# A chain of transformer layers: the score buffers in PSUM as single banks instead of pairs of banks

## The chip, the cores and the metric

The kernel runs on one core of a Trainium2 chip. The metric is the device time of one execution. The kernel before took 545.48 us (median of three runs, 543.8 to 546.18). The profiled execution that all traces below come from has a span of 545.9 us. Engines are called by their names in the profile: PE is TensorE (PEld its weight loads), DVE VectorE, ACT ScalarE, POOL GpSimd, SP the queue that issues DMA.

## The reference, cut to what matters

The input x has 8 sequences of 256 tokens with 128 features, all float32. Eight residual blocks follow each other, each on the layernorm of x:

```
x = x + causal_attention(ln(x))      # one head
x = x + ffn_relu(ln(x))
x = x + linear_attention(ln(x))
x = x + ffn_relu(ln(x))
x = x + retention(ln(x))             # 16 heads
x = x + ffn_silu(ln(x))
x = x + softmax_attention(ln(x))     # 16 heads of 8 features
x = x + ffn_silu(ln(x))
```

The change concerns the softmax attention of 16 heads:

```
scores = einsum('bhqd,bhkd->bhqk', q, k) / sqrt(8)
attn = softmax(scores)
ctx = einsum('bhqk,bhkd->bhqd', attn, v)
out = ctx @ Wo.T + bo
```

So there are 8 sequences x 16 heads, each with a 256 x 256 matrix of scores.

## The kernel before, in words

**Groups.** The 8 sequences are cut into 4 groups of 2. Each group walks through all layers (`layers`, L1253) as a thread of its own, and the groups start a little apart, so that at any time different groups are in different layers and their work mixes on the engines. The last group ends alone.

**Who sets the order.** The order of instructions is worked out in Python, before anything runs, by `Plan` (L111). Every piece of work is a generator that yields steps such as `step(DVE, 1.15)`: an engine and a booked time in us. The planner holds a clock for each engine, adds a handoff time when work goes from one engine to another, and always emits the step that can start first; among those that could start, the thread with the lower rank goes first (group 0 ahead of group 3; the scores of the softmax attention, rank -1, ahead of all). The booked times decide only the order of instructions in each engine's queue. On the chip each engine works through its queue in that order and waits on semaphores for its data and buffers.

**Buffers.** Buffers lie in stores. A thread that wants one yields `get(store, n)` and gets it when the planner thinks that it is free; `put` gives it back, with `later=LEEWAY` 0.4 us after the planned end. PSUM has eight banks of 512 float32 columns for each partition. Before the change they are four tiles of two banks, the twins (L338); all other work takes single halves of twins from the store `bank` (L340).

**Scores.** `pairs_of_scores` (L1026) is one endless thread that serves all softmax attentions. Scores are computed twice: first with queries on the partitions, to find the maximum of each row (`firsts`), and then, with the negative maximum joined to the operands as one more row, with keys on the partitions, for the exponential (`seconds`). The unit is a pair of heads, `(seq, h2)`: two matmuls for each head, one for each 128 rows of its score matrix, so four in all. They are float32, and each shows as two records in the profile, so a pair is x8 at L1070. Each uses 32 rows of the array. A head's rows, `place(h)` (L1023), are one of four groups of 32 rows; a pair takes two of them. A step of the planner takes one pair (a lone step) or two pairs on different rows, booked with 0.8 us of PE either way (L1065).

While other groups are under way, two twins are lent to the scores, and a step with two pairs waits for both (L1056). Once the last group is in its softmax attention, `todo["alone"]` is set, a third twin is lent (L1036), and a step takes the first twin that comes free. A second pair joins only if another twin is free at that moment (L1060); otherwise it goes back to its queue.

**After the scores.** `maxima` (L1085) takes the negative maximum of both heads with one DVE instruction over the whole twin, 1024 columns, and gives the twin back. After four pairs, the maxima are transposed, copied and sent by DMA into the rows of the operands, and the four pairs go to `seconds`. `exponentials` (L1119) takes the exponential of both heads with one ACT instruction over the twin, into a buffer `probs`, and gives the twin back. `weighted` (L1128) multiplies the probabilities of four pairs with the values (L1140); the column of ones in the values gives the sums of the softmax. When all is done for a sequence, the output projection (L1237) and the second `ffn_silu` follow, for that sequence alone.

Of the kernel before, what the change touches and what calls it, by code (L numbers as in the profile page):

```python
# [27 lines left out]
F32 = mybir.dt.float32  # L28
I32 = mybir.dt.int32
AF = mybir.ActivationFunctionType  # L30
ALU = mybir.AluOpType
AX = mybir.AxisListType

P = 128
B, S, D = 8, 256, 128
GROUPS = 4
NT = 4
N = NT * P
# [22 lines left out]
PE, ACT, DVE, POOL, SP = "pe", "act", "dve", "pool", "sp"  # L61
# [3 lines left out]
LEEWAY = 0.4  # L65
# [45 lines left out]
class Plan:  # L111
# [18 lines left out]
    def spawn(self, steps, rank=None):  # L130

        c = self.current
        th = Thread(steps, c.rank if rank is None else rank, c.t if c else 0.0, c.last if c else None)
        self.resume(th, None)
        return th
# [8 lines left out]
    def put(self, store, *items, later=0.0):  # L144
        for item in items:
            self.count += 1
            store.items.append((self.current.after() + later, self.count, item))
# [94 lines left out]
def step(engine, us, table=None):  # L242
    return ("step", ((engine, us, table),))
# [6 lines left out]
def get(store, n=1):  # L250
    return ("get", store, n)
# [6 lines left out]
def until(condition):  # L258
    return ("until", condition)


def wake(us):
    return ("at", us)
# [3 lines left out]
def hybrid(ctx: ExitStack, tc: tile.TileContext, t: dict, out: bass.AP):  # L267
    nc = tc.nc
    plan = Plan()
    put, spawn = plan.put, plan.spawn  # L270
# [3 lines left out]
    psum = ctx.enter_context(tc.tile_pool(name="psum", bufs=1, space=bass.MemoryType.PSUM))  # L274
# [4 lines left out]
    def buffers(name, n, shape):  # L279
        return plan.store([buffer(f"{name}{i}", shape) for i in range(n)])  # L280
# [54 lines left out]
    plan.free[POOL], plan.free[ACT] = 2.6, 2.6  # L335


    twins = [psum.tile([P, 2, N], F32, tag=f"twin{i}", name=f"twin{i}") for i in range(4)]  # L338
    halves = [[tw[:, k, :] for k in range(2)] for tw in twins]
    bank = plan.store([h for pair in halves for h in pair], strict=True)  # L340
    twin = plan.store([])
    work = buffers("work", 28, [P, WORK])
    small = buffers("small", 16, [P, P])
    probs = buffers("probs", 6, [P, 2, N])
# [15 lines left out]
    def flat(tl):  # L360
        return tl.rearrange("p a b -> p (a b)")
# [8 lines left out]
    def copied(dst, src, us):  # L370
        e = yield either((ACT, us), (DVE, us + 0.02))
        (nc.scalar.copy if e == ACT else nc.vector.tensor_copy)(dst, src)  # L372
# [644 lines left out]
        pass  # L1017

    firsts, seconds = deque(), deque()
    todo = {"sequences": 2 * GROUPS, "banks": [0, 1], "alone": False}  # L1020
    under_way = [0, 0]

    def place(h):  # L1023
        return slice(32 * (h % 4), 32 * (h % 4) + 32), h // 4

    def pairs_of_scores():  # L1026

        yield until(lambda: firsts)
        yield get(bank, halves[0] + halves[1])
        put(twin, *twins[:2])
        while todo["sequences"]:
            yield until(lambda: firsts or seconds or not todo["sequences"])
            if todo["alone"] and len(todo["banks"]) == 2:  # L1036
                yield get(bank, halves[2])
                put(twin, twins[2])
                todo["banks"].append(2)
            chosen = []  # L1040
            kinds = [(firsts, 0), (seconds, 1)]
            if todo["alone"] and under_way[0] > under_way[1]:
                kinds.reverse()
            for queue, of_keys in kinds + kinds:
                for n in range(min(2, len(queue))):
                    if len(chosen) == 2 or any(h2 % 2 == queue[n][1] % 2 for _, _, h2 in chosen):
                        continue
                    if n and queue[0][1] // 2 != queue[1][1] // 2:
                        continue
                    chosen.append((of_keys, *queue[n]))  # L1050
                    del queue[n]
                    break
            if not chosen:
                break
            if len(chosen) == 2 and not todo["alone"]:
                ps = yield get(twin, 2)  # L1056
            else:
                ps = [(yield get(twin))]
                if len(chosen) == 2:
                    if any(i[0] <= plan.now for i in twin.items):  # L1060
                        ps.append((yield get(twin)))
                    else:
                        of_keys, *pair = chosen.pop()
                        (seconds if of_keys else firsts).appendleft(tuple(pair))
            yield step(PE, 0.8)  # L1065
            for n in range(2):
                for k in range(2):
                    for (of_keys, seq, h2), to in zip(chosen, ps):
                        rows, j = place(2 * h2 + k)
                        nc.tensor.matmul(  # L1070
                            to[:, k, n * S : (n + 1) * S],
                            seq.spread[rows, j, of_keys, n * P : (n + 1) * P],
                            seq.spread[rows, j, 1 - of_keys, :], start=True, stop=True,
                        )
            for (of_keys, seq, h2), to in zip(chosen, ps):
                under_way[of_keys] += 1
                if of_keys:
                    seq.scored += 1
                    if seq.scored == HEADS // 2:
                        put(l_spread, seq.spread)  # L1080
                spawn((exponentials if of_keys else maxima)(seq, h2, to))
        yield get(twin, twins[: len(todo["banks"])])
        put(bank, *[h for n in todo["banks"] for h in halves[n]])

    def maxima(seq, h2, ps):  # L1085
        half = h2 // 4
        flat_nmax = seq.nmax[:, 16 * half : 16 * half + 16]
        nmax = flat_nmax.rearrange("p (j i m) -> p j i m", i=4, j=2)
        yield step(DVE, 1.15)
        nc.vector.tensor_reduce(  # L1090
            nmax[:, h2 % 4 // 2, 2 * (h2 % 2) : 2 * (h2 % 2) + 2, :],
            ps.rearrange("p k (m s) -> p k m s", m=2), AX.X, ALU.max, negate=True,
        )
        put(twin, ps, later=LEEWAY)
        under_way[0] -= 1
        seq.found[half] += 1
        if seq.found[half] < 4:
            return

        rows = yield get(small)  # L1100
        ps = yield get(bank)
        yield step(PE, 0.12)
        nc.tensor.transpose(ps[:16, :P], flat_nmax, ident)
        seq.turned += 1
        if seq.turned == 2:
            put(small, seq.nmax)
        yield from copied(rows[:16, :], ps[:16, :P], 0.25)
        put(bank, ps)
        for j in range(2):
            yield step(SP, 0.5)  # L1110
            nc.sync.dma_start(
                seq.spread[KDIM:P:32, 2 * half + j, 0, :], rows[8 * j : 8 * j + 8, :]
            )
        put(small, rows)
        yield wake(plan.current.after())
        seconds.extend((seq, 4 * half + n) for n in range(4))
        seq.parts.append(spawn(weighted(seq, half)))

    def exponentials(seq, h2, ps):  # L1119

        p = yield get(probs)
        yield step(ACT, 1.05, "exp")
        nc.scalar.activation(flat(p), flat(ps), AF.Exp)  # L1123
        put(twin, ps, later=LEEWAY)
        under_way[1] -= 1
        seq.p[h2] = (p, plan.current.after())

# [140 lines left out]
    plan.start(silu_weights(), LAST, 24.0)  # L1268
    plan.start(softmax_weights(), LAST, 24.0)
    plan.start(pairs_of_scores(), FIRST, 0.0)  # L1270
    plan.run()
    return plan
# [108 lines left out]
```

## Time and profile before

| What | Value |
|---|---|
| median of three runs | 545.48 us |
| span of the trace | 545.9 us |
| PE busy | 468.9 us, 86% |
| DVE busy | 343.6 us, 63% |
| ACT busy | 225.5 us, 41% |
| score matmuls L1070 | 1024 records, 99.3 us of PE |
| maxima L1090 | 64 instructions, 76.3 us of DVE |
| exponentials L1123 | 64 instructions, 63.4 us of ACT |
| first score matmul | at 210.8 us |
| mean granted PE clock | 0.934 of full speed |

A group's line in the profile gives line, engine, operation, destination <- sources, shapes and count; then the busy time in us and the mean of one instruction in ns; then how long the engine sat idle just before these instructions and which instruction released most of it. A line of a stage gives the stage, its length, the busy time of PE, PEld, DVE, ACT and POOL with the number of instructions in brackets, the granted PE clock as a share of full speed, and DMA. A line of the timeline gives the start and the length of a run of equal instructions, and their count at the end; idle time before it stands in square brackets. Line numbers are those of the kernel before. The helper `copied` records all its copies at L372.

### The profile page before, as it was taken

The numbers are of one execution on the slowest core, as the hardware profiler recorded it, in microseconds if no ns is written. First come the engines' busy times: TensorE is split into PE (matmuls) and PEld (weight loads), VectorE is DVE, ScalarE is ACT, GpSimd is POOL, SyncE is SP. The second block draws the span as 40 slices with busy tenths as digits, with TensorE's granted clock in tenths as the row PEclk, the third lists the DMA queues.
The fourth block names the chain that finished last, engine by engine and source line by source line (L and its number), as shares of the span: only waits on it lengthen the run. The fifth ranks groups of instructions, "written<-read, shape, count | busy, mean of one in ns | idle before, by whom it ended". The sixth has DMA issues, their size and how long they took to land. (4 is left out here: it accounts for less than half of the span.)

```text
span 545.9 us, 12836 instructions
## 1 busy us (share of the span) xinstructions
PE 468.9 (86%) x5340; PEld 316.8 (58%) x5340; DVE 343.6 (63%) x911; ACT 225.5 (41%) x414; POOL 146.1 (27%) x260
## 2 busy tenths in 40 slices
PE   2788799798889898899888788899779998989986
PEld 1676577566656666355654554556547565656555
DVE  6978774987795759776428874543876542752023
ACT  3235354432433242345443246435434664122362
POOL 6705476683352522415000120220001030000000
PEclk9979989999899989899989889989999999965599
DMA  8000000002002010002101002001000002000000
GB/s 297 37 2 1 1 1 1 0 18 26 3 14 27 3 42 2 1 2 40 25 3 22 2 18 24 3 22 24 2 1 22 10 13 41 11 1 11 2 0 20
DMA packets 8041, 10.88 MB, mean 20 GB/s; under 512 B 1000, under 2 KB 6888, under 8 KB 7984
## 3 DMA queue, kind: packets, MB, share of 16 engines
q1 hardware_dynamic: 7904, 9.94, 7.9%
q8 instruction: 42, 0.69, 0.6%
q14 instruction: 15, 0.12, 0.1%
q10 hardware_dynamic: 80, 0.13, 0.1%
HBM read 4.56 MB, written 1.05 MB: 10 GB/s over the span
## 5 line engine op out<-in xcount | busy, mean ns | idle before, releaser
L1070 PE MATMUL twin<-l_spread 32*128 32x256 f32 x1024 | 99.3, 443 | 3.9 <-DVE small L1090 3.3
L1090 DVE TENSOR_REDUCE small<-twin 128x4 f32<-128x1024 f32 x64 | 76.3, 1218 | 25.0 <-PE twin L1070 24.9
L470 POOL TENSOR_SCALAR small<-small 128x4 f32<-128x4 f32 (+1 forms) x44 | 10.4, 237 | 288.5 <-DVE small L468 287.5
L1123 ACT ACTIVATE probs<-twin 128x1024 f32<-128x1024 f32 x64 | 63.4, 1023 | 57.1 <-PE twin L1070 56.2
L372 ACT COPY work<-twin 128x512 f32<-128x512 f32 (+3 forms) x80 | 37.9, 481 | 114.4 <-PE twin L1140 30.5
L1070 PEld LDWEIGHTS twin<-l_spread 32*128 32x128 f32 x1024 | 62.7, 206 | 33.1 <-issue 15.3
L372 DVE COPY work<-twin 128x512 f32<-128x512 f32 (+3 forms) x32 | 17.6, 554 | 44.3 <-PE twin L1140 19.6
L1140 PE MATMUL twin<-probs,l_values 128*32 128x256 f32 x512 | 38.9, 444 | 7.2 <-DVE work L780 2.7
L472 POOL TENSOR_TENSOR small<-small,mhalf 128x4 f32<-128x4 f32 (+1 forms) x44 | 43.2, 982 | 0.0
L479 ACT ACTIVATE work<-x,small 128x128 f32<-128x128 f32 x74 | 32.3, 487 | 25.1 <-POOL small L473 24.9
L499 PE MATMUL twin<-ident,work 128*128 128x128 f32 x128 | 24.8, 299 | 16.8 <-ACT work L479 9.6
L467 DVE BATCH_NORM_STATS2 small<-x 128x6 f32<-128x128 f32 x128 | 34.5, 270 | 4.5 <-DMA x<-in_x 4.2
L484 DVE TENSOR_SCALAR work<-x,small 128x128 f32<-128x128 f32 x54 | 29.4, 765 | 6.3 <-POOL small L472 6.2
L468 DVE BATCH_NORM_AGGREGATE small<-small 128x2 f32<-128x6 f32 x160 | 29.1, 182 | 5.6
L659 PE MATMUL twin<-work,c_relu 128*128 128x512 f32 x64 | 30.5, 603 | 1.8 <-ACT work L372 1.8
L672 PE MATMUL twin<-c_relu,work 128*128 128x128 f32 x256 | 31.5, 277 | 0.1
L672 PEld LDWEIGHTS twin<-c_relu,work 128*128 128x128 f32 x256 | 30.1, 192 | 2.7 <-issue 1.4
L1140 PEld LDWEIGHTS twin<-probs,l_values 128*32 128x32 f32 x512 | 16.5, 123 | 25.5 <-issue 10.1
L499 PEld LDWEIGHTS twin<-ident,work 128*128 128x128 f32 x128 | 15.3, 145 | 27.2 <-ACT work L479 16.4
L985 PE MATMUL twin<-work,c_ints 128*128 128x256 f32 (+1 forms) x72 | 26.6, 489 | 4.3 <-ACT work L372 1.5
L1001 PE MATMUL twin<-c_ints,work 128*128 128x128 f32 x192 | 28.2, 294 | 2.0 <-DVE x L522 1.2
L991 PE MATMUL twin<-work,c_ints 128*128 128x256 f32 (+1 forms) x72 | 26.3, 485 | 2.8 <-DVE work L929 1.2
(145 smaller groups left out, 794.2 us busy)
## 6 DMA issues: line engine op xcount, KB each, us to landing
r_spread<-wide SPq DMA_DIRECT2D x32, 64.0 KB
l_spread<-wide SPq DMA_DIRECT2D x32, 64.0 KB
out<-x SPq DMA_DIRECT2D x8, 128.0 KB
c_retention_qk<-in_retention_qk SPq DMA_DIRECT2D x1, 770.0 KB
x<-in_x SPq DMA_DIRECT2D x3, 256.0 KB
c_retention_vo<-in_retention_vo SPq DMA_DIRECT2D x1, 713.0 KB
c_relu<-in_relu SPq DMA_DIRECT2D x1, 706.0 KB
c_ints<-in_ints SPq DMA_DIRECT2D x1, 576.0 KB
```

Source lines behind the costliest of these rows:

```text
L372: (nc.scalar.copy if e == ACT else nc.vector.tensor_copy)(dst, src)
L467: nc.vector.bn_stats(stats[:, i, :], src[:, i, :])
L472: nc.gpsimd.tensor_tensor(rstd, rstd, minus_half[:, :nt], ALU.pow)
L479: nc.scalar.activation(y[:, i, :], src[:, i, :], AF.Identity, bias=shift[:, i : i + 1], scale=rstd[:, i : i + 1],)
L484: nc.vector.tensor_scalar(y[:, i, :], src[:, i, :], mv[:, i, 0:1], rstd[:, i : i + 1], ALU.subtract, ALU.mult,)
L499: nc.tensor.transpose(ps[:, i * P : (i + 1) * P], y[:, i, :], ident)
L659: nc.tensor.matmul(ps, w1[:, c * P : (c + 1) * P], yT[:, :N], start=True, stop=True)
L672: nc.tensor.matmul(ps[:, n * D : (n + 1) * D], h[c][:, i * P : (i + 1) * P], w2[:, c, :], start=(c == 0), stop=(c == 3),)
L1070: nc.tensor.matmul(to[:, k, n * S : (n + 1) * S], seq.spread[rows, j, of_keys, n * P : (n + 1) * P], seq.spread[rows, j, 1 - of_keys, :], ...
L1090: nc.vector.tensor_reduce(nmax[:, h2 % 4 // 2, 2 * (h2 % 2) : 2 * (h2 % 2) + 2, :], ps.rearrange("p k (m s) -> p k m s", m=2), AX.X, ALU.m ...
L1123: nc.scalar.activation(flat(p), flat(ps), AF.Exp)
L1140: nc.tensor.matmul(o[32 * i : 32 * (i + 1), (j % 2) * S : (j % 2 + 1) * S], seq.v[:, c, VONE * h : VONE * h + 32], seq.p[h2][0][:, k, c * ...
```

## The change

The four twins become eight tiles of one bank each. A pair of heads now gets two such tiles, any two, one for each head. The maximum and the exponential are taken by one instruction for each head, of 512 columns instead of 1024, and each gives its bank back as soon as it has ended, instead of both together. The lending changes from two (later three) twins to four (later six) banks: outside the tail a step with two pairs waits for four banks; in the tail a step waits for two, and a second pair joins if two more are free at that moment. What it is for: finer buffers, so that a bank is not held for the sake of its neighbour, and a reader can start when one head is there. The planner's booked times go from 1.15 to 2 x 0.61 us for a maximum and from 1.05 to 2 x 0.6 us for an exponential. The matmuls, their order inside a step, and the arithmetic stay as they are.

```diff
-    twins = [psum.tile([P, 2, N], F32, tag=f"twin{i}", name=f"twin{i}") for i in range(4)]
-    halves = [[tw[:, k, :] for k in range(2)] for tw in twins]
-    bank = plan.store([h for pair in halves for h in pair], strict=True)
-    twin = plan.store([])
+    banks = [psum.tile([P, N], F32, tag=f"bank{i}", name=f"bank{i}") for i in range(8)]
+    bank = plan.store(banks, strict=True)
+    score_bank = plan.store([])
...
-            if todo["alone"] and len(todo["banks"]) == 2:
-                yield get(bank, halves[2])
-                put(twin, twins[2])
-                todo["banks"].append(2)
+            if todo["alone"] and todo["banks"] == 4:
+                yield get(bank, banks[4:6])
+                put(score_bank, *banks[4:6])
+                todo["banks"] = 6
...
             if len(chosen) == 2 and not todo["alone"]:
-                ps = yield get(twin, 2)
+                ps = yield get(score_bank, 4)
             else:
-                ps = [(yield get(twin))]
+                ps = yield get(score_bank, 2)
                 if len(chosen) == 2:
-                    if any(i[0] <= plan.now for i in twin.items):
-                        ps.append((yield get(twin)))
+                    if sum(i[0] <= plan.now for i in score_bank.items) > 1:
+                        ps = ps + (yield get(score_bank, 2))
                     else:
...
+            ps = [ps[n : n + 2] for n in range(0, len(ps), 2)]
...
-                            to[:, k, n * S : (n + 1) * S],
+                            to[k][:, n * S : (n + 1) * S],
...
     def maxima(seq, h2, ps):
-        yield step(DVE, 1.15)
-        nc.vector.tensor_reduce(
-            nmax[:, h2 % 4 // 2, 2 * (h2 % 2) : 2 * (h2 % 2) + 2, :],
-            ps.rearrange("p k (m s) -> p k m s", m=2), AX.X, ALU.max, negate=True,
-        )
-        put(twin, ps, later=LEEWAY)
+        for k in range(2):
+            yield step(DVE, 0.61)
+            nc.vector.tensor_reduce(
+                nmax[:, h2 % 4 // 2, 2 * (h2 % 2) + k, :],
+                ps[k].rearrange("p (m s) -> p m s", m=2), AX.X, ALU.max, negate=True,
+            )
+            put(score_bank, ps[k], later=LEEWAY)
...
     def exponentials(seq, h2, ps):
-        yield step(ACT, 1.05, "exp")
-        nc.scalar.activation(flat(p), flat(ps), AF.Exp)
-        put(twin, ps, later=LEEWAY)
+        for k in range(2):
+            yield step(ACT, 0.6, "exp")
+            nc.scalar.activation(p[:, k, :], ps[k], AF.Exp)
+            put(score_bank, ps[k], later=LEEWAY)
```

More of the change, by code (lines that the diff above doesn't have):

```diff
@@ L1019, in hybrid @@
     firsts, seconds = deque(), deque()
-    todo = {"sequences": 2 * GROUPS, "banks": [0, 1], "alone": False}
+    todo = {"sequences": 2 * GROUPS, "banks": 4, "alone": False}
     under_way = [0, 0]
@@ L1031, in pairs_of_scores @@
         yield until(lambda: firsts)
-        yield get(bank, halves[0] + halves[1])
-        put(twin, *twins[:2])
+        yield get(bank, banks[:4])
+        put(score_bank, *banks[:4])
         while todo["sequences"]:
             yield until(lambda: firsts or seconds or not todo["sequences"])
-            if todo["alone"] and len(todo["banks"]) == 2:
-                yield get(bank, halves[2])
-                put(twin, twins[2])
-                todo["banks"].append(2)
+            if todo["alone"] and todo["banks"] == 4:
+                yield get(bank, banks[4:6])
+                put(score_bank, *banks[4:6])
+                todo["banks"] = 6
             chosen = []
@@ L1081, in pairs_of_scores @@
                 spawn((exponentials if of_keys else maxima)(seq, h2, to))
-        yield get(twin, twins[: len(todo["banks"])])
-        put(bank, *[h for n in todo["banks"] for h in halves[n]])
+        yield get(score_bank, todo["banks"])
+        put(bank, *banks[: todo["banks"]])
     def maxima(seq, h2, ps):
```

## The prediction

> **What bounds the kernel now.** I read the page's engine totals first, then the busy tenths, the chain that ended last, the granted clock by stage, and last the timeline of the tail.
>
> ```profile
> PE 468.9 (86%) x5340; PEld 316.8 (58%) x5340; DVE 343.6 (63%) x911; ACT 225.5 (41%) x414; POOL 146.1 (27%) x260
> ...
> PEclk9979989999899989899989889989999999965599
> ...
> PE twin L1070 10%; PE twin L1140 5%; PE twin L1001 3%; PE twin L991 3%; DVE small L1090 2%; PE twin L985 2%; PE twin L1153 1%; DVE work L993 1%; PE twin L527 1%; DVE x L522 1%; PE twin L1182 1%; ACT L987 1%; PE twin L499 1%; PE twin L938 1%; PE twin L853 1%
> ...
> L1090 DVE TENSOR_REDUCE small<-twin 128x4 f32<-128x1024 f32 x64 | 76.3, 1218 | 25.0 <-PE twin L1070 24.9
> ...
> L1123 ACT ACTIVATE probs<-twin 128x1024 f32<-128x1024 f32 x64 | 63.4, 1023 | 57.1 <-PE twin L1070 56.2
> ```
>
> TensorE is busy 86% of the span and carries most of the chain. The two groups that the change cuts in half, L1090 and L1123, stand mostly behind it: they wait 24.9 and 56.2 us for the score matmuls of L1070. The other way round, L1070 matmuls wait only 3.3 us, four times, for L1090 (chain of waits). On the chain in order of time L1090 has 2.4% of 545.9, so 13.1 us, 10.8 of its 64 instructions.
>
> The busy time by stage (columns: PE, PEld, DVE, ACT, POOL, then the clock) shows where TensorE is slow rather than waiting:
>
> ```profile
> 210.00:464.00 254.00, 220.07 (x2864) 140.44 (x2864) 154.59 (x364) 116.14 (x186) 39.73 (x74) 0.97 0.08 15
> 464.00:481.00 17.00, 15.79 (x121) 9.94 (x120) 14.26 (x16) 4.09 (x9) 1.33 (x4) 1.00 0.03 9
> 481.00:518.50 37.50, 36.98 (x206) 22.16 (x207) 8.58 (x13) 10.66 (x13) 0.00 (x0) 0.50 0.02 5
> ```
>
> From 210 to 464 us, where scores of groups 0 to 2 run among other groups' layers, TensorE is 87% busy, VectorE 61%, ScalarE 46%. Before 210 there is no score at all, so nothing changes there. From 481 to 518.5 TensorE is full at half clock: the last group is alone, and the half clock costs 36.98 / 2 = 18.5 us.
>
> The timeline of TensorE and VectorE in the tail shows the grain:
>
> ```profile
> 472.38 1.13 PE L1070 MATMUL twin<-l_spread 32*128 32x256 f32 x8
> ...
> 475.76 2.00 PE L1070 MATMUL twin<-l_spread 32*128 32x256 f32 x24
> 478.22 2.26 PE L1070 MATMUL twin<-l_spread 32*128 32x256 f32 x16 [0.46 <-DVE small L1090]
> ...
> 490.67 2.08 PE L1070 MATMUL twin<-l_spread 32*128 32x256 f32 x8
> ```
>
> ```profile
> 465.57 5.75 DVE L1090 TENSOR_REDUCE small<-twin 128x4 f32<-128x1024 f32 x5 [0.66 <-PE twin L1070]
> ...
> 476.94 3.49 DVE L1090 TENSOR_REDUCE small<-twin 128x4 f32<-128x1024 f32 x3 [0.47 <-PE twin L1070]
> ```
>
> A step with one pair of heads (x8) takes 1.06 us on the chain; in the middle stage a step with two pairs (x16) takes 1.07 us. So a lone pair wastes half a step, and at half clock a lone step is 2.0 us. The last group has 256 score matmuls, 32 pairs of heads. Its score time is 11.93 us (464 to 481), 23.50 (481 to 518.5) and 3.41 (after): 11.93/1.065 + 23.50/2.02 + 3.41/1.07 = 26 steps. So only some 6 steps hold two pairs and 20 hold one.
>
> [...] matmuls on different row groups of the array run at the same time; the 1.06 and 1.07 us agree. [...] from 481 on TensorE is busy and stays at 0.50 for 37 us: busy time alone doesn't lift it here. [...] A twin is two banks, each used alone by other work already, so eight separate tiles take no necessary wait away; no line of this trace shows a wait between two halves. [...]
>
> **The change part by part.** *Maximum in two halves.* Rows with a PSUM source on VectorE: 128x256 takes 418 ns (L522), 128x512 takes 685 (L372), 128x1024 takes 1218 (L1090). The slope is 1.04 ns per element, the fixed part 0.15 us, so a half should take 0.685 and two of them 1.37, which is 0.15 more. Back to back the instructions overlap: five reduces take 5.75 us, 1.15 each, so the fixed part that a queue feels is about 1.15 - 1.07 = 0.08. VectorE gains 64 x 0.08 to 0.15 = 5 to 10 us of work. On the path stand 10.8 of them: 0.9 to 1.6 us. I take **+1.2**.
>
> *Exponential in two halves.* ScalarE's copy of 128x512 takes 586 ns (L372), so two halves 1.17 against 1.02; three exponentials in a row took 2.85 us, against 3.07 one by one, so two halves in a row cost 0.04 to 0.15 more. ScalarE is below half busy, and the chain in order of time shows it at two full exponentials in the stretch from 423 to 454 and few elsewhere: 0.1 to 0.4 us, I take **+0.2**. The rest lies behind L1070.
>
> *Waits on TensorE.* A score step now writes tiles whose last readers may be different instructions, on different engines: the store hands out the two tiles that come free first. L1070 has 29 semaphore instructions of 51 ns on the weight-load queue, 1.5 us. They become 29 to 58: 0 to 1.5, I take **+0.8**. Queued behind a waiting L1070 on TensorE is all other groups' work; those who wait for it are L1090 and L1123.
>
> *Earlier release.* The first half of a pair comes free after 0.69 instead of 1.22 us. Where L1070 waits for L1090 (four times) that can save at most 4 x 0.53 = 2.1 us; nothing if all four tiles must be free, as outside the tail they must. I take **-0.8**. The first half's reader also starts one or two matmuls sooner, off the path.
>
> *The planner.* It books 2 x 0.61 for a maximum (before 1.15) and 2 x 0.6 for an exponential (before 1.05), and the release rule changes. So from 210 us on the order of everything is drawn anew. In the tail a lone step needs any two free tiles of six, which are there sooner, for instance a half from VectorE and a half from ScalarE; a second pair joins only if two more are free at that moment. Sooner means rather alone: I expect 25 to 29 score steps instead of 26, each worth 1.06 us at full and 2.0 at half clock. The stretch where VectorE holds TensorE up (476.9 to 480.4) gets longer, and the clock falls at its end. I book one more window of about 3.4 us at half clock, **+1.7**; bounds -9 (half of the 18.5 gone) and +8 (four more lone steps).
>
> The rest (slices for tiles, the lending and the return of banks) moves no instruction; it is hidden behind TensorE.
>
> Sum: 1.2 + 0.2 + 0.8 - 0.8 + 1.7 = +3.1, **548.6 us**.
>
> **The rivals.** *Nothing to see*, 545.5: TensorE is the bound from 210 to 464, VectorE has 39% to spare there, and the extra 5 to 10 us fill waits of 24.9 us. Against it: the order cannot stay as it is, and the tail is sensitive. *Faster*, 539: the finer store lets TensorE run on, or pairs meet more often: three lone steps fewer at 2.0 (-6.0), two windows at half clock fewer (-3.4), against +2.2 for the instructions and waits, gives 538.3; with a saving in the middle stage left at nothing, I say 539. For it: the half-clock stretch of 37.5 us is most of what the tail can have, so a new order has more to win than to lose there. Against: the rule favours lone steps. *Much slower*, 556: four more lone steps at 2.0 (+8.0) and +2.2 for instructions and waits, 555.7. For it: 20 of 26 steps are lone already; against: TensorE's other work in the tail lets tiles gather.
>
> **How the numbers follow.** Forecast (546.5 to 552) 0.42, nothing 0.18, faster 0.27, much slower 0.13. The bound of 0.5% is 2.7 us, so 548.2 parts same from slower; some 0.08 of the forecast case lies below it. Faster 0.27, same 0.26, slower 0.34 + 0.13 = 0.47. The range 539.5 to 556 leaves out the outer parts of both outer cases, about 2 in 10, and covers the bounds on the tail short of their extremes.
>
> **What would show it.** Of the steps: 128 reduces of about 0.685 us and 128 exponentials of about 0.59; VectorE's total up by about 10 us as sum of durations and ScalarE's likewise; TensorE's score time at full clock unchanged; the same trace up to 210 us; more semaphore instructions before L1070's weight loads. The tail would show 25 to 29 score steps and a clock of 0.50 for 37 to 41 us. The prediction is wrong if the half-clock stretch goes or shrinks by half, if many lone steps become double, or if the planner's new order opens or closes gaps of TensorE in the middle stage (34 us now) by more than 3 us.

## The result, and the profile after

The changed kernel took 515.6 us (median of four runs, 509.34 to 516.47) against 544.64 us: ratio 0.945, 95% interval 0.936 to 0.954. That is 5.5% faster, where 548.6 us was forecast. The median of the kernel before moved between 539.7 and 546.4 us in the sets of runs below, so each kernel is judged by its ratio to the runs beside it. Some executions run at a lower granted clock and take longer (the kernel before, in one set: 542.11 us at 0.939, 555.79 at 0.917); the medians include them, the ratios leave them out.

The page of the changed kernel, with the lines that answer to those of before:

```profile
span 514.7 us, 13048 instructions
...
PE 465.5 (90%) x5340; PEld 320.9 (62%) x5340; DVE 354.2 (69%) x985; ACT 238.9 (46%) x477; POOL 144.4 (28%) x259
...
PEclk9979989999989999969999999999979999655899
...
PE bank L1071 16%; PE bank L1143 6%; PE bank L659 5%; PE bank L985 5%; DVE small L1092 4%; PE bank L1001 4%; PE bank L991 4%; PE bank L672 3%; PE bank L795 3%; DVE work L484 3%; PE bank L853 3%; PE bank L499 2%; DVE small L467 2%; PE bank L527 2%; DVE small L468 2%
...
L1092 DVE TENSOR_REDUCE small<-bank 128x2 f32<-128x512 f32 x128 | 80.3, 682 | 27.8 <-PE bank L1071 27.6
L1126 ACT ACTIVATE probs<-bank 128x512 f32<-128x512 f32 x128 | 68.0, 599 | 48.3 <-PE bank L1071 44.7
```

TensorE does the same work in almost the same time, 465.5 us against 468.9. VectorE and ScalarE do more, 10.6 and 13.4 us. What went is idle time of TensorE: 545.9 - 468.9 = 77.0 us before, 514.7 - 465.5 = 49.2 after. The mean granted clock is the same (0.934 and 0.933), so the clock does not make the gain.

Where it went shows in the busy time by stage: up to the first score matmul, from there to the last one, and the rest. Before:

```profile
0.00:210.80 210.80, 176.48 (x1988) 130.35 (x1988) 158.66 (x498) 82.46 (x188) 102.45 (x174) 0.96 0.12 31
210.80:525.20 314.40, 278.74 (x3258) 176.16 (x3258) 178.13 (x392) 135.50 (x212) 41.06 (x78) 0.91 0.07 13
525.20:545.90 20.70, 13.70 (x98) 10.29 (x96) 6.80 (x22) 7.56 (x15) 2.63 (x8) 1.00 0.04 13
```

After:

```profile
0.00:203.70 203.70, 174.27 (x1989) 130.23 (x1989) 159.83 (x498) 84.22 (x188) 101.79 (x174) 0.97 0.13 32
203.70:494.90 291.20, 276.76 (x3253) 180.50 (x3254) 186.51 (x463) 148.38 (x276) 39.95 (x77) 0.91 0.07 14
494.90:514.70 19.80, 14.51 (x102) 10.15 (x98) 7.84 (x25) 6.30 (x13) 2.64 (x8) 0.97 0.04 14
```

TensorE's idle time (stage minus the first busy time) falls from 34.3 to 29.4, from 35.7 to 14.4, and from 7.0 to 5.3 us. The first stage is the telling one. It ends with the first score, and in it the compiled programs of both kernels list the same instructions in the same order. They use the same banks, too; only the tiles to which the banks belong differ, and the waits. Still the stage is 7.1 us shorter. No halved reduce, no early release and no new order can do that. It is no accident of one profile: with four twins the first score starts at 210.8, 213.2 and 209.0 us (before and two of the kernels below), with eight tiles at 203.7, 204.2, 205.0 and 202.7.

A wait that names the cause stands in the old profile. L1161 is a VectorE reciprocal on a bank that only the transposes of L1153 have written. What its engine sat idle for, in the kernel before:

```profile
L1161 DVE RECIPROCAL small<-twin x16: 247/258/259, 256.2 to 529.7; 128x16 f32<-128x16 f32 x16
...
  PE twin L1001: 5.5, 2
  PE twin L853: 5.2, 1
  ACT probs L1123: 2.8, 1
  ACT work L890: 2.6, 1
  PE twin L1153: 2.0, 1
```

And the same instruction (L1164, its transposes L1156) in the changed kernel:

```profile
L1164 DVE RECIPROCAL small<-bank x16: 246/258/259, 249.7 to 499.2; 128x16 f32<-128x16 f32 x16
...
  PE bank L1156: 11.4, 9
  ACT probs L1126: 2.8, 1
```

Before, it is released mostly by matmuls of the feed-forward (L1001) and the retention (L853) of other groups, with which it shares no data; its own producer has the last of these lines. After, it waits for its producer. The compiled programs agree: before, 8 of the 16 reciprocals are made to wait for work in the other bank of their twin; after, none is. (The wait put down to L1126 stands in no compiled wait of L1164; the profile infers releasers.) The timeline of one such place in the kernel before:

```profile
370.26 0.66 PE L1153 MATMUL twin<-ident,work 128*128 128x128 f32 x4
...
370.85 0.86 PE L853 MATMUL twin<-work,r_values 64*32 64x64 f32 x64
...
371.80 0.26 DVE L1161 RECIPROCAL small<-twin 128x16 f32<-128x16 f32 x1 [5.21 <-PE twin L853]
```

The transposes are over at 370.92, the reciprocal starts at 371.80, 0.1 us after a stranger's last matmul. In the compiled program this reciprocal reads bank 7, and the L853 matmul that it waits for writes bank 6, the other half of the same tile.

### The profile page after: what moved, and what is told of

Same layout as the page of the kernel before. It is cut to its first block, busy times and chain, and to the rows that moved or that the text cites. A ratio compares the mean times of both kernels' runs of the same rounds, so it can differ in the third digit from the quotient of the medians.

```text
span 514.7 us, 13048 instructions
## 1 busy us (share of the span) xinstructions
PE 465.5 (90%) x5340; PEld 320.9 (62%) x5340; DVE 354.2 (69%) x985; ACT 238.9 (46%) x477; POOL 144.4 (28%) x259
## 3 DMA queue, kind: packets, MB, share of 16 engines
HBM read 4.56 MB, written 1.05 MB: 11 GB/s over the span
## 4 chain that ended last, share of the span: by engine, by line
PE 69%; DVE 22%; issue 3%; POOL 2%; ACT 1%; DMA 1%; SPq 0%; POOLq 0%; DVEq 0%; ACTq 0%
PE bank L1071 16%; PE bank L1143 6%; PE bank L659 5%; PE bank L985 5%; DVE small L1092 4%; PE bank L1001 4%; PE bank L991 4%; PE bank L672 3%; PE bank L795 3%; DVE work L484 3%; PE bank L853 3%; PE bank L499 2%; DVE small L467 2%; PE bank L527 2%; DVE small L468 2%
## 5 line engine op out<-in xcount | busy, mean ns | idle before, releaser
L1071 PE MATMUL bank<-l_spread 32*128 32x256 f32 x1024 | 104.3, 443 | 3.6 <-DVE small L1092 3.2
L1092 DVE TENSOR_REDUCE small<-bank 128x2 f32<-128x512 f32 x128 | 80.3, 682 | 27.8 <-PE bank L1071 27.6
L1126 ACT ACTIVATE probs<-bank 128x512 f32<-128x512 f32 x128 | 68.0, 599 | 48.3 <-PE bank L1071 44.7
L1071 PEld LDWEIGHTS bank<-l_spread 32*128 32x128 f32 x1024 | 66.7, 205 | 33.1 <-issue 12.9
L372 ACT COPY work<-bank 128x512 f32<-128x512 f32 (+3 forms) x76 | 36.2, 481 | 85.6 <-PE bank L499 24.7
L372 DVE COPY work<-bank 128x512 f32<-128x512 f32 (+3 forms) x36 | 19.8, 555 | 26.2 <-PE bank L1143 12.8
L499 PE MATMUL bank<-ident,work 128*128 128x128 f32 x128 | 25.1, 306 | 12.5 <-ACT work L479 9.3
L484 DVE TENSOR_SCALAR work<-x,small 128x128 f32<-128x128 f32 x57 | 30.4, 747 | 5.9 <-POOL small L472 5.9
L1143 PE MATMUL bank<-probs,l_values 128*32 128x256 f32 x512 | 33.6, 398 | 0.2 <-DVE work L780 0.2
L985 PE MATMUL bank<-work,c_ints 128*128 128x256 f32 (+1 forms) x72 | 30.0, 535 | 3.5 <-ACT work L372 1.6
L659 PE MATMUL bank<-work,c_relu 128*128 128x512 f32 x64 | 31.5, 617 | 0.9 <-ACT work L372 0.9
L672 PEld LDWEIGHTS bank<-c_relu,work 128*128 128x128 f32 x256 | 30.1, 192 | 2.6 <-issue 1.9
L672 PE MATMUL bank<-c_relu,work 128*128 128x128 f32 x256 | 31.4, 277 | 0.1
L499 PEld LDWEIGHTS bank<-ident,work 128*128 128x128 f32 x128 | 15.7, 149 | 23.2 <-ACT work L479 13.6
L1001 PEld LDWEIGHTS bank<-c_ints,work 128*128 128x128 f32 x192 | 23.9, 191 | 5.7 <-issue 3.2
L1001 PE MATMUL bank<-c_ints,work 128*128 128x128 f32 x192 | 26.7, 283 | 0.8 <-DVE work L993 0.8
```

The lines of the kernel that those rows point to most:

```text
L484: nc.vector.tensor_scalar(y[:, i, :], src[:, i, :], mv[:, i, 0:1], rstd[:, i : i + 1], ALU.subtract, ALU.mult,)
L499: nc.tensor.transpose(ps[:, i * P : (i + 1) * P], y[:, i, :], ident)
L659: nc.tensor.matmul(ps, w1[:, c * P : (c + 1) * P], yT[:, :N], start=True, stop=True)
L672: nc.tensor.matmul(ps[:, n * D : (n + 1) * D], h[c][:, i * P : (i + 1) * P], w2[:, c, :], start=(c == 0), stop=(c == 3),)
L985: nc.tensor.matmul(ps[:, :n], w_gate[:, cols], yT[:, :n], start=True, stop=True)
L1001: nc.tensor.matmul(ps[:, (i - first) * D : (i - first + 1) * D], h[c][:, i * P : (i + 1) * P], w_down[:, c, :], start=(c == 0), stop=(c == 2),
```

## Experiments

**Theory S (sharing).** Two banks in one tile are one thing to the code that sets the semaphores. An instruction on one bank is made to wait for the last reader or writer of the other, though the work there is a stranger's. **Theory F (fine release).** Banks that come free one by one, with the new order that follows, make the gain. A third possibility is that the split itself, two short instructions for one wide one, is good.

**The new order on old tiles.** The changed kernel, with its eight banks as views of two-bank tiles:

```diff
-    banks = [psum.tile([P, N], F32, tag=f"bank{i}", name=f"bank{i}") for i in range(8)]
+    twins = [psum.tile([P, 2, N], F32, tag=f"twin{i}", name=f"twin{i}") for i in range(4)]
+    banks = [tw[:, k, :] for tw in twins for k in range(2)]
```

> The changed kernel, with its order of instructions and its halved maxima and exponentials, but the eight banks are views of four two-bank tiles as before. Theory S (sharing: with two banks in one tile, the code that sets the semaphores makes work in one bank wait for readers or writers of the other bank): the gain is gone, 538 to 552 us, TensorE idle about 75 us, first score matmul near 211 us. Theory F (the gain comes from banks that come free one by one and from the new order): 510 to 520 us, first score matmul near 204.

Measured: 557.56 us, ratio 1.028 (1.017 to 1.038). The order on TensorE and VectorE is that of the changed kernel to the last instruction, and the first score matmul starts at 209.0 us. The gain is gone and turned into a loss of 3%, more than either theory gave (552 us at most under S). F falls: fine release and new order, without separate tiles, cost time. TensorE's idle time is back:

```profile
span 553.5 us, 12976 instructions
...
PE 474.9 (86%) x5340; PEld 318.2 (57%) x5340; DVE 353.6 (64%) x985; ACT 236.8 (43%) x477; POOL 144.3 (26%) x259
```

**The old order on new tiles.** The kernel before, its planner untouched (a maximum is booked as one step of 1.15, both banks go back together), on eight tiles:

```diff
-    twins = [psum.tile([P, 2, N], F32, tag=f"twin{i}", name=f"twin{i}") for i in range(4)]
-    halves = [[tw[:, k, :] for k in range(2)] for tw in twins]
+    banks = [psum.tile([P, N], F32, tag=f"bank{i}", name=f"bank{i}") for i in range(8)]
+    twins = halves = [banks[2 * i : 2 * i + 2] for i in range(4)]
...
+        for k in range(2):
             nc.vector.tensor_reduce(
-                ... ps.rearrange("p k (m s) -> p k m s", m=2), ...
+                ... ps[k].rearrange("p (m s) -> p m s", m=2), ...
```

(the target of the score matmuls and the exponential likewise).

> The kernel before with its order of instructions and its joint release of both banks, but on eight tiles of one bank; a maximum or exponential is two instructions in a row. Theory S: 513 to 524 us, first score matmul near 204 us, TensorE idle about 50 us. Theory F: 543 to 555 us, since nothing comes free earlier and the instructions cost more.

Measured: 509.57 us, ratio 0.939 (0.929 to 0.949). All of the gain, a little more than S gave (513 us at least), with neither the new release nor the new order. Its stages:

```profile
0.00:205.00 205.00, 175.95 (x1989) 131.47 (x1989) 159.34 (x498) 84.40 (x188) 101.81 (x174) 0.95 0.12 32
205.00:487.50 282.50, 269.33 (x3255) 176.23 (x3254) 181.45 (x456) 139.46 (x273) 41.13 (x78) 0.92 0.08 15
487.50:507.60 20.10, 14.73 (x106) 10.67 (x98) 6.83 (x22) 8.02 (x17) 2.63 (x8) 1.00 0.04 14
```

In the middle stage TensorE idles 282.5 - 269.3 = 13.2 us, as in the changed kernel (14.4).

**The split alone.** Two-bank tiles, the old order, each maximum and exponential as two instructions in a row:

```diff
     halves = [[tw[:, k, :] for k in range(2)] for tw in twins]
+    twins = halves
```

> The kernel before, two-bank tiles, same order, with each maximum and exponential as two instructions. It prices the split alone: the prediction's 1.2 + 0.2 us, so 544 to 550 us in every theory. If it were below 540, the split itself would be the gain.

Measured: 542.37 us beside 546.37, ratio 1.003 (0.998 to 1.007). By the ratio that is 1.5 us, between -0.9 and 3.8; the median itself lies just below the 544 to 550 that were expected. The split is no gain; it costs little or nothing.

This kernel and the one above emit the same instructions in the same order on the same banks on every engine, so their compiled programs can be compared wait by wait. I counted the waits on TensorE, VectorE and ScalarE that ask more of another of these engines than the waiter's queue had asked already, and whether the instruction waited for touches the waiter's bank:

```
waiter      waits that ask more   of these: later than on eight tiles, and the instruction
on twins                          waited for touches only the other bank of the twin
PE          507                   252
DVE         323                   199
ACT         320                   176
```

Of 1150 waits 627 are for the neighbour. About a third of them (217) lie between the score matmuls and their own maxima and exponentials, that is, inside the twins that are lent to the scores; the rest tie strangers together. This goes in both directions: matmuls into one bank wait for readers of the other (L499 for L567, for instance), and readers wait for matmuls into the other (L372 for L527; line numbers of the kernel before). The program on eight tiles holds more semaphore waits in all (769 against 636 on TensorE): I read it so that a wait for a stranger is late enough to make several right ones unnecessary. Fewer waits are no sign of looser coupling.

**Which banks matter.** Two kernels in the old order cut the sharing in half. In the first, the two pairs of banks that are lent to the scores stay two-bank tiles with wide instructions, and the other four are single (with two instructions where the tail lends a pair of them to the scores):

```diff
-    twins = [psum.tile([P, 2, N], F32, tag=f"twin{i}", name=f"twin{i}") for i in range(4)]
-    halves = [[tw[:, k, :] for k in range(2)] for tw in twins]
+    twins = [psum.tile([P, 2, N], F32, tag=f"twin{i}", name=f"twin{i}") for i in range(2)]
+    banks = [psum.tile([P, N], F32, tag=f"bank{i}", name=f"bank{i}") for i in range(4)]
+    halves = [[tw[:, k, :] for k in range(2)] for tw in twins] + [banks[:2], banks[2:]]
+    twins = twins + halves[2:]
```

> The kernel before in its order; the two twins that are lent to the scores stay two-bank tiles with one instruction for both heads, the other four banks are single tiles. Theory S: sharing stays only in the first 210 us on half of the banks, and between the two heads of a score pair: 518 to 530 us, first score matmul at 205 to 209. Theory F: no change, 543 to 549.

Measured: 501.08 us, ratio 0.922 (0.914 to 0.929), faster than S gave it (518 to 530): the sharing that is left here costs nothing that can be seen. It was run again beside the changed kernel:

> The kernel before in its order, two two-bank tiles for the scores with one wide instruction for each pair of heads, four single tiles for the rest. Again on the same chip as the others: 499 to 504 us, 2% to 3% below the changed kernel, with a profile of an undisturbed execution.

Measured: 505.88 us, ratio 0.936 (0.927 to 0.946). And the changed kernel beside it:

> The changed kernel unaltered, beside the two below on one chip. 510 to 517 us. Theory S gives all of its gain to the eight separate tiles and nothing to banks that come free one by one: then the kernel with the old order and joint release on eight tiles is not slower than it. Theory F's rest (separate release worth some us in the tail) would put this one ahead.

Measured: 509.36 us, ratio 0.937 (0.928 to 0.946). So the kernel with score twins is as fast as the changed one. That it is 2% faster, as I expected, the second set doesn't show. Splitting its wide instructions:

```diff
-        if isinstance(ps, list):
+        if True:
             for k in range(2):
```

> As the kernel with two score twins and four single tiles, same order, but each maximum and exponential in two instructions. It prices the split where TensorE is 90% busy. From the durations VectorE and ScalarE get 5 us each more, most of it hidden: 501 to 505 us. If the split is what makes eight single tiles slower than score twins, 507 to 511.

Measured: 510.95 us, ratio 0.939 (0.928 to 0.951), not to be told from the wide one. (The median lies in the second of the ranges that were expected, that of a split that costs; the interval does not decide between the two.)

The complement has single tiles for the scores and two twins for all other work (and for the third pair of the tail):

```diff
-    halves = [[tw[:, k, :] for k in range(2)] for tw in twins] + [banks[:2], banks[2:]]
-    twins = twins + halves[2:]
+    halves = [banks[:2], banks[2:]] + [[tw[:, k, :] for k in range(2)] for tw in twins]
+    twins = halves[:2] + twins
```

> The complement of the kernel with score twins: the order of the kernel before, the four banks that are lent to the scores are single tiles, the other four stay two twins. Theory S: from the first score on, the two heads of a pair are read and written by the same few instructions anyway, so sharing hurts where two strangers lie in one tile, in the other four banks: most of the loss stays, 528 to 540 us, first score at 206 to 209. If the scores' own banks were the sore point: 505 to 515.

Measured: 538.1 us, ratio 0.990 (0.980 to 1.000). So some 1%, perhaps nothing, lies in the scores' own tiles and 6% in the other four banks, where two strangers share a tile: the third of the wrong waits that lies within the scores is not the dear one. The first score starts at 210.3 us, not at the expected 206 to 209; with score twins it started at 206.7, though half of the banks are shared there, too, and the runs don't say why. In this kernel the reciprocal waits for strangers still (L1003 is the feed-forward, L855 the retention, L1166 its own transposes):

```profile
L1174 DVE RECIPROCAL small<-twin x16: 246/258/259, 254.4 to 520.4; 128x16 f32<-128x16 f32 x16
...
  PE twin L1003: 5.5, 2
  PE twin L855: 3.6, 1
  ACT work L892: 2.6, 1
  PE twin L1166: 2.4, 2
```

With single tiles there, in the kernel with score twins, only for its transposes:

```profile
L1174 DVE RECIPROCAL small<-bank x16: 246/257/258, 247.6 to 492.3; 128x16 f32<-128x16 f32 x16
...
  PE bank L1166: 16.5, 8
```

**The tail.** All kernels so far keep TensorE at half clock for 17.1 to 41.0 us after the last group is alone, and there most steps are lone. The prediction had the clock fall after a stretch in which VectorE holds TensorE up (before, one such stretch ends at 480.4 us, and half clock begins at 480.9), and counted lone steps as time wasted at that clock. On top of the kernel with score twins, a step with two pairs now waits for both twins in the tail, too:

```diff
-            if len(chosen) == 2 and not todo["alone"]:
+            if len(chosen) == 2:
```

> As the kernel with two score twins and four single tiles, but in the tail, too, a step waits until two pairs have room, so 16 steps of two pairs in place of 26 lone ones and 3 double ones. If lone steps are what fills TensorE at half clock in the tail: 13 steps of 1 to 2 us fewer, [...] 478 to 492 us. If the waits for two free twins cost as much as they save: 497 to 505.

Measured: 492.41 us, at the upper end of what was expected, ratio 0.913 (0.906 to 0.920); beside it the kernel with score twins had 505.88 (0.936). The tail of that one, up to, at and after half clock:

```profile
430.70:443.90 13.20, 13.20 (x90) 8.29 (x92) 11.15 (x13) 2.79 (x6) 0.00 (x0) 0.99 0.01 2
443.90:481.40 37.50, 37.50 (x211) 22.19 (x209) 9.59 (x17) 11.29 (x17) 0.00 (x0) 0.50 0.02 5
481.40:487.80 6.40, 6.40 (x75) 4.03 (x75) 1.52 (x5) 4.45 (x6) 0.00 (x0) 1.00 0.00 0
```

With double steps only:

```profile
430.70:443.90 13.20, 12.80 (x109) 7.99 (x109) 11.83 (x17) 2.77 (x7) 0.00 (x0) 1.00 0.04 12
443.90:457.60 13.70, 12.94 (x89) 7.67 (x91) 4.36 (x5) 5.72 (x10) 0.00 (x0) 0.50 0.01 2
457.60:472.70 15.10, 14.14 (x184) 8.40 (x181) 5.17 (x9) 10.37 (x16) 0.00 (x0) 1.00 0.01 2
```

The last score ends at 472.7 instead of 487.8 us. The score matmuls of these stages take 25.3 us of TensorE in place of 37.7, and half clock lasts 13.7 us in place of 37.5. That is one profiled execution against one, and lone steps don't always hold the clock so long: in the kernel with the split alone and in the complement, with the same 26 lone steps as before, half clock in the tail lasted 17.1 us, in the others 27.3 to 41.0. In the traces of before and after the granted clock takes two values only, 1.00 and 0.50 (22 and 14 stretches), so the mean granted clock of an execution gives its time at half clock, by estimate 2 x (1 - clock) x span: 46 us on average of the four executions with lone steps, 25 with double ones. The direction holds, with a smaller difference. The same edit on the changed kernel (a step of two pairs waits for four banks):

> The changed kernel, but in the tail, too, a step of two pairs waits for four banks. 16 double steps in place of 28 lone and 2 double. If the lone steps feed the half clock here as with the score twins: 2% to 4% below the changed kernel, 490 to 502 us, half clock in the tail 10 to 20 us in place of 27 to 37.

Measured: 497.01 us, ratio 0.918 (0.911 to 0.925), with 10.2 us of half clock in the tail (whole executions, by the same estimate: 35 us, where the changed kernel had 62 and 52 in its two sets). Both beat the kernels before and after.

## Why the prediction was wrong

The forecast had the wrong sign because of what it left at nothing. By its own steps:

*Tiles: the step that failed.* The prediction said that "eight separate tiles take no necessary wait away; no line of this trace shows a wait between two halves", and that the rest "moves no instruction; it is hidden behind TensorE". The first clause holds: no necessary wait went. But 627 of 1150 waits were not necessary, and removing such waits was worth the whole gain, shown by the swap in both directions (0.939 with new tiles alone, 1.028 with all but new tiles). With it fell "Before 210 there is no score at all, so nothing changes there": that stage became 7.1 us shorter. The mark that it set itself, 3 us of TensorE's gaps in the middle stage, was passed by far. That the semaphores keep engines apart by single banks was the author's assumption; the compiled programs set them by tiles, which on twins gave those 627. And the trace did show the waits: L1161 behind L1001 and L853 is in the list of waits of before, with 5.5 and 5.2 us. The forecast took from that list the lines that the change touches, not releasers that have no data in common with the waiter. The rival *faster* had the sign and nearly nothing else: 539 us, from pairs that meet more often.

*"TensorE is the bound" was half of it.* 87% busy from 210 to 464 us left 34 us of idle time, and the forecast asked only how the new instructions would fit into it, not what caused it. In the stage from the first score to the last, 21 of 36 us went.

*The maximum.* Forecast 0.685 us for a half, measured 0.682. *The exponential:* 0.586 forecast, 0.599 measured. The sum for the split, +1.4 us, agrees with the 1.5 measured, whose interval includes nothing at all.

*Waits on TensorE.* L1071 has 34 semaphore instructions of 51 ns where L1070 had 29: 0.3 us, where +0.8 was taken.

*Earlier release.* -0.8 was taken. The old joint release on new tiles (0.939) is not slower than the new one (0.945 and 0.937), so it is worth nothing that these runs can tell. The bound of 2.1 us had counted the matmuls of L1070 alone; their weight loads waited 6.6 us more for L1090. Neither wait shrank to speak of: 3.3 and 6.6 us before, 3.2 and 8.0 after.

*The planner and the tail.* +1.7 us was taken for one more window at half clock (in the trace of before, eight of the ten whole stretches at half clock last 3.41 us each); half clock in the tail lasted 37.5 us in the profiles before and after (27.3 in a second profile of the changed kernel). On twins the new order costs 3%, which no term had and these runs don't explain; on eight tiles that cost isn't seen. The compiled programs hold 26 lone and 3 double steps before, 28 and 2 after. From the busy time the forecast had made 20 and 6, because lone steps that follow each other on other rows overlap: the x24 that it shows at 475.76 is three lone steps in 2.00 us, where one takes 1.06. So 29 steps became 30, where it said 25 to 29. That the rule favours lone steps was right. That lone steps cost time in the tail is shown by the double ones, with both tiles. That they keep the clock low is shown in part: half clock in the tail lasted 17.1 to 41.0 us with lone steps, 13.7 and 10.2 with double ones. What in the double steps ends it sooner, these runs do not tell.

## What to carry to other kernels

Let a tile be the unit that one owner holds: if strangers work in two parts of one tile, the waits that are set for them tie them together, and what stands behind the waiter in its engine's queue pays too: at the place shown, L484 on VectorE started at 372.30 us, behind the reciprocal, on an operand that POOL had written by 368.00. In a profile look for releasers that did not produce what the waiter reads; the line of the releaser, not the length of the wait, gives it away. What counts is who shares: two heads of one pair in a tile cost 1% or nothing here, strangers 6%. Idle time of the engine that bounds the kernel needs a cause before a change is priced against it.

## What the runs showed of the hardware that was not expected

TensorE stayed at half clock for 37.5 us while it was busy all the time (37.50 of 37.50 us in the kernel with score twins): in that tail busy time alone did not bring the full clock back. Nor did idle time come before the fall of the clock in that kernel: TensorE had been busy for 13.20 of the 13.20 us before it, as the profile counts it. With lone steps it returned after 17.1 to 41.0 us in ten profiles, with double ones after 13.7 and 10.2 in two.
